# Perceiver megakernel, one core: PSUM banks of the first passes in two fixed sets, keys and values apart, one positive part on VectorE

## The chip, the cores and the metric

The kernel runs on one core of a Trainium2 chip. The metric is the device time of one execution in microseconds (us). Engines are named as the profile names them: PE (TensorE matmul) with PEld (its weight loads), DVE (VectorE), ACT (ScalarE), POOL (GpSimd), SP (the queue that issues most DMAs).

## The reference, cut to what matters

Four layers run one after the other on 128 tokens of width 256. Each has a cross attention over 12,544 context tokens of width 192, a self attention and a mixture of experts. The change lies in the cross attentions of the first three layers, all of this form (16 heads of width 16; the first has a mask, the second and third have biases, the second clips the scores):

```
q = (x @ Wq + bq)          # 128 x 256, in 16 heads
k = (context @ Wk + bk)    # 12544 x 256
v = (context @ Wv + bv)
scores = einsum(q, k) * scale
attn = softmax(scores, axis=-1)      # over 12544 keys
out  = einsum(attn, v);  x = x + out @ Wo + bo
```

## The kernel before, in words

`attend_twice` goes over the keys twice for each of two groups of eight heads: a first pass finds each row's highest score, a second pass (not touched) takes exponentials and weights the values. Three layers times two groups make six first passes.

A first pass has 25 steps, one for each pair of a pair of key blocks and a head half (a block is 512 context tokens, 25 blocks, the last half full). PE, DVE and ACT each keep the order in which the work is written down (`in_order`); POOL and SP do not. One step has four parts on PE, called K, V, O and H from here on:

- **K**: `keys.project(part 0)`, line 112: keys of a later block, 6 matmuls of 256 columns, on two row halves of the array.
- **V**: `keys.project(part 1)`, line 112: its values, 12 matmuls of 128 columns. After V, `keep` copies both out of PSUM: ACT takes the first half's keys and values (lines 145 or 147, 154), DVE the second half's (141 or 143, 152).
- **O**: `over`, line 641: queries times the difference of two key blocks (made by POOL, `apart`), 4 products of 512 columns t0 to t3, one on each 32-row quarter of the array. Line 672: ACT takes the positive part (Relu) of each into SBUF.
- **H**: `highest_of_two`, line 641, for the O of the step before: queries times the second block, 4 products. Line 678: DVE adds the positive part and keeps the maximum, four custom instructions ("customs").  With a mask (first layer), each H product begins with a bf16 matmul of a mask row (line 640).

So the highest of two blocks costs one maximum: max(a, b) = b + relu(a - b).

Which steps have K and V is set by `steps`. In the first layer and in every second group, almost every step projects a block; its last three projections have keys only (`values` is false for the last three blocks), the two steps after them have none. In the first group of the second and third layers eight blocks are there already, and every fourth step has no K and V. The values that are left out are projected at the end (`project_values`): those of block 22 just before the last H.

All of these products lie in one pool of 8 PSUM banks that go round (`single`: one bank of [128, 512] f32). A full step takes ten: K and V of a block share two (keys in the first half of each bank, values in the second), O four, H four. A matmul into a bank waits until the last reader of what lay there is done. Going round, this means in a full step: K's two banks are those of t0 and t1 of the O before; O's are those of t2 and t3 of the O before and t0 and t1 of the H before; H's are the last two of the H before and the K, V banks of its own step.

## Time and profile before

| | us |
|---|---|
| median of 3 runs (lowest, highest) | 3015.29 (3006.1, 3017.43) |
| the profiled execution's own time | 3019.33 |
| its span, first to last instruction | 3017.6 |
| PE busy in the span | 2877.8 |
| DVE busy | 2024.6 |
| ACT busy | 1691.3 |

The first passes lie, with what begins and ends them, in about 31 to 158, 281 to 410, 640 to 780, 915 to 1041, 1320 to 1455 and 1563 to 1693 us of the span: 787 us together, of which PE is busy for 766. Since matmuls are pipelined and their ends are modelled, that busy share says little on how near to its limit PE is; the distance from one O to the next tells the length of a step. It is read here in the timeline, from the first weight load of line 641 in a step, or from the first of the four rows of line 678.

### The profile page before, as it was taken

Reading aid. Unit: us, or ns where it says so; the run is one execution under the profiler, and the core shown is the slowest. Engines: PE = TensorE matmul, PEld = TensorE weight load, DVE = VectorE, ACT = ScalarE, POOL = GpSimd, SP = SyncE. Lnnn points to the kernel's source line nnn. Section 1 sums busy time; section 2 is a strip of 40 time slices with the busy share of each in tenths; the row PEclk is TensorE's granted clock in tenths of the full one; section 3 lists DMA queues with packets and bytes.
Section 4 is the critical chain, followed back from the end, with each engine's and each line's share of the span. In section 5 each row is a group of like instructions: output and inputs, shape, how many; then the busy total and the mean of one; then the engine's idle time right before and its main releaser. Section 6 shows DMA issues by size and latency. Waiting matters only on the chain.

```text
span 3017.6 us, 83446 instructions
## 1 busy us (share of the span) xinstructions
PE 2877.8 (95%) x36469; PEld 2250.9 (75%) x36469; DVE 2024.6 (67%) x3720; ACT 1691.3 (56%) x2326; POOL 288.4 (10%) x356
## 2 busy tenths in 40 slices
PE   8999999989999999899999998899999999999979
PEld 5677767456677676776777675688988989889858
DVE  4676677525895797657556655577777777777844
ACT  3577568234685585235775682355655656555521
POOL 4401420123001100121001002000000000000000
PEclk9999999899999998899999998999999999999979
DMA  5301310461002202431112007232223222222436
GB/s 156 92 19 42 108 34 26 175 224 53 21 3 76 68 5 87 132 117 48 32 34 76 27 4 261 87 97 83 85 78 88 85 78 88 81 82 84 135 115 199
DMA packets 149888, 255.32 MB, mean 85 GB/s; under 512 B 17892, under 2 KB 88159, under 8 KB 149524
## 3 DMA queue, kind: packets, MB, share of 16 engines
q1 hardware_dynamic: 144774, 235.01, 25.0%
q0 software_dynamic: 3744, 14.16, 1.5%
q8 instruction: 287, 4.70, 0.6%
q10 hardware_dynamic: 1006, 0.82, 0.1%
q14 instruction: 77, 0.63, 0.1%
HBM read 249.74 MB, written 0.19 MB: 83 GB/s over the span
## 4 chain that ended last, share of the span: by engine, by line
PE 74%; DVE 7%; ACT 2%; DMA 2%; POOL 1%; issue 1%; SPq 0%; DVEq 0%; POOLq 0%; ACTq 0%
PE acc L791 8%; PE pair L205 8%; PE one L641 8%; PE v L205 8%; PE one L112 7%; PE sc L949 6%; PE acc L991 5%; PE pair L721 5%; PE ps L329 4%; PE one L721 3%; PE acc L329 2%; PE pair L714 2%; PE kv L112 2%; PE ps L1787 1%; DVE sums L340 1%
## 5 line engine op out<-in xcount | busy, mean ns | idle before, releaser
L678 DVE CUSTOM_DVE_ANT_0 over<-over,one 128x512 f32<-128x512 f32 x576 | 361.0, 684 | 174.6 <-PE one L641 170.6
L672 ACT ACTIVATE over<-one 128x512 f32<-128x512 f32 x576 | 298.3, 602 | 92.5 <-PE one L641 84.8
L205 PEld LDWEIGHTS v<-wv,ctx 64*128 64x128 f32 (+1 forms) x3136 | 295.2, 190 | 12.0 <-issue 1.9
L205 PE MATMUL v<-wv,ctx 64*128 64x128 f32 (+1 forms) x3136 | 300.4, 274 | 0.0
L951 ACT COPY kept<-sc 128x1024 f32<-128x1024 f32 (+1 forms) x135 | 136.2, 1009 | 261.1 <-PE sc L949 261.1
L205 PE MATMUL pair<-ctx,wk 64*128 64x256 f32 (+1 forms) x1440 | 276.0, 384 | 1.2 <-ACT kT L233 1.1
L641 PE MATMUL one<-apart,qz 32*128 32x512 f32 x1536 | 246.6, 635 | 16.2 <-POOL apart L662 9.0
L340 DVE TENSOR_TENSOR top<-top,kept 128x1024 f32<-128x1024 f32 (+2 forms) x145 | 169.1, 1169 | 133.6 <-ACT kept L951 132.3
L343 DVE SCALAR_TENSOR_TENSOR e<-pair,floor 128x1024 f32<-128x1024 f32 x196 | 226.4, 1217 | 12.0 <-PE pair L721 12.0
L112 PEld LDWEIGHTS one<-ctx,wk 64*128 64x128 f32 x1464 | 156.9, 190 | 99.5 <-ACT over L672 84.7
L769 ACT ACTIVATE e<-pair 128x1024 f32<-128x1024 f32 x196 | 200.9, 1025 | 52.0 <-PE pair L721 29.8
L746 ACT ACTIVATE e<-e 128x1024 f32<-128x1024 f32 x196 | 207.4, 1058 | 33.1 <-DVE e L343 22.4
L721 PE MATMUL pair<-qz,kT 32*128 32x256 f32 x2112 | 218.9, 374 | 0.0
L205 PEld LDWEIGHTS pair<-ctx,wk 64*128 64x128 f32 (+1 forms) x1440 | 192.3, 188 | 34.1 <-issue 13.2
L112 PE MATMUL one<-ctx,wk 64*128 64x256 f32 x1464 | 214.8, 400 | 0.7 <-DVE o L340 0.7
L791 PE MATMUL acc<-e,v 128*17 128x128 f32 x6336 | 211.4, 274 | 3.0 <-ACT e L784 2.2
L112 PEld LDWEIGHTS one<-wv,ctx 64*128 64x128 f32 x2928 | 207.4, 193 | 8.8 <-ACT over L672 4.5
L112 PE MATMUL one<-wv,ctx 64*128 64x128 f32 x2928 | 208.3, 278 | 0.0
L791 PEld LDWEIGHTS acc<-e,v 128*17 128x17 f32 x6336 | 155.8, 97 | 67.8 <-ACT e L784 45.2
L784 ACT ACTIVATE e<-e 128x1024 f32<-128x1024 f32 x196 | 205.0, 1048 | 0.0
L343 DVE SCALAR_TENSOR_TENSOR e<-one,maskcol,less 128x256 f32<-128x256 f32 x392 | 162.6, 477 | 53.1 <-PE one L721 43.0
L949 PE MATMUL sc<-qz,kT 64*128 64x128 f32 x2816 | 197.8, 279 | 0.0
(479 smaller groups left out, 5271.7 us busy)
## 6 DMA issues: line engine op xcount, KB each, us to landing
ctx<-in_ctx SPq DMA_DIRECT2D x132, 384.0 KB
ctx<-in_ctxA SPq DMA_DIRECT2D x198, 256.0 KB
w<-in_L_ffn_W SPq DMA_DIRECT2D x32, 1024.0 KB
ctx<-in_ctxB SPq DMA_DIRECT2D x207, 128.0 KB
w<-in_L_ffn_w_gateT SPq DMA_DIRECT2D x8, 1024.0 KB
wu<-in_L_ffn_w_upT SPq DMA_DIRECT2D x8, 1024.0 KB
w<-in_L_ffn_w_downT SPq DMA_DIRECT2D x8, 1024.0 KB
w<-in_L_ffn_w1T SPq DMA_DIRECT2D x8, 1024.0 KB
```

Source lines behind the costliest of these rows:

```text
L112: self.nc.tensor.matmul(out, a, b, start=first, stop=last, skip_group_check=True)
L205: self.nc.tensor.matmul(out, a, b, start=start and not low, stop=low == 1, skip_group_check=True)
L343: self.nc.vector.scalar_tensor_tensor(out, a, s, b, op0, op1, **kw)
L641: nc.tensor.matmul(x, qz[r, g, s, :], k[r, :n], start=row is None, stop=True)
L672: nc.scalar.activation(e, x, AF.Relu)
L678: nc.vector.tensor_tensor_reduce(es[t], es[t], x, 1.0, -LARGEST, ALU.add, ALU.max, parts[:, s, t, i : i + 1])
L721: nc.tensor.matmul(at, keys.kT(c // 4)[tiles[t], k], q, start=start, stop=True, skip_group_check=True)
L746: nc.scalar.activation(to, to, AF.Exp)
L769: nc.scalar.activation(to, pair, AF.Exp)
L784: nc.scalar.activation(to, to, AF.Exp)
L791: nc.tensor.matmul(acc[32 * t : 32 * t + 17, half, :], v[:, c % 4 + j, 4 * half + t, :], es[half][:, t // 2, j, t % 2, :], start=c + j + h ...
L949: nc.tensor.matmul(x[:, t, c : c + P], kT[r, c : c + P], qz[r, g, :], start=True, stop=True)
```

## The change

1. The eight banks get fixed numbers and two sets of four, `free` (0 to 3 at first) and `taken` (4 to 7), which change parts after every step and after each of the blocks projected ahead. In a step, keys lie in the first two banks of `free`, values in the other two, O in the four of `taken`, and H in the four of `free` again. So after the change K and V wait for the four positive parts of the O before (K for t0 and t1, V for t2 and t3), O waits for the four customs of the H before (one each), and H for the copies of keys and values of its own step.
2. Keys and values have banks of their own, and both key copies go to ACT (`keep_keys`); they wait for K alone, no longer for V. DVE keeps one copy, that of the second half's values.
3. In steps that project something (`shared`), DVE takes the positive part of t1 with a `tensor_scalar` maximum with 0, in its order after the copy of values and before the customs; ACT takes three. Counted over the program, 124 of 576 positive parts move from ACT to DVE and 119 key copies of 128x256 move from DVE to ACT. PE, POOL and SP issue the same instructions as before, PE and POOL in the same order; on SP a load of a mask row and one of a context block change places.
4. Everything else that takes banks in the first pass (`project_values`, the last block's maxima, `lowered` and others) still goes round through all eight, with a counter of its own.

```diff
+    def keep_keys(self, g, b, p):
+        for i, _ in self.halves(b):
+            to, k = self.kT(b)[:, i * HB : (i + 1) * HB], p[:, i, :HB]
+            if self.bias is None:
+                self.nc.scalar.copy(to, k)
+            else:
+                self.nc.scalar.activation(to, k, AF.Identity, bias=self.bias[:, g : g + 1])
...
-            p = self.started[g, b] = self.net.early_two() if self.rest is None else self.net.two()
+            if self.rest is None:
+                p = self.net.early_two()
+            elif self.net.split:
+                p = self.net.banks_of(self.net.free[:2])
+            else:
+                p = self.net.two()
+            self.started[g, b] = p
             self.keys_into(p, g, b)
             return
         p = self.started[g, b]
-        if values:
-            self.values_into(p, g, b, HB)
-        self.keep(g, b, p, values=values)
+        if self.rest is not None and self.net.split:
+            if values:
+                v = self.net.banks_of(self.net.free[2:4])
+                self.values_into(v, g, b)
+            self.keep_keys(g, b, p)
+            if values:
+                self.keep(g, b, v, 0, keys=False)
+        else:
+            if values:
+                self.values_into(p, g, b, HB)
+            self.keep(g, b, p, values=values)
...
+        self.free, self.taken = list(range(4)), list(range(4, 8))
...
     def single(self):
+        if self.split:
+            self.next = (self.next + 1) % 8
+            return self.bank(self.next)
         return self.pone.tile([P, SB], F32, tag="one", name="one")
+
+    def bank(self, i):
+        return self.pone.tile([P, SB], F32, tag=f"one{i}", name="one", bufs=1)
+
+    def banks_of(self, at):
+        return Banks([self.bank(i) for i in at])
...
-            xs = [self.single()[:, :n] for _ in range(4)]
+            xs = [(self.single() if at is None else self.bank(at[t]))[:, :n] for t in range(4)]
...
-            for e, x in zip(out, products(g, 2 * i, s, less[0])):
-                nc.scalar.activation(e, x, AF.Relu)
+            for t, (e, x) in enumerate(zip(out, products(g, 2 * i, s, less[0], at=at))):
+                if shared and t == 1:
+                    self.ts(e, x, 0.0, None, ALU.max)
+                else:
+                    nc.scalar.activation(e, x, AF.Relu)
...
                 for b in range(lead):
                     for low in range(2):
                         keys.project(g, b, low)
+                    self.free, self.taken = self.taken, self.free
...
-                    es = over(g, i, s, less) if b < NSB - 1 else None
+                    es = over(g, i, s, less, self.taken, bool(steps[b])) if b < NSB - 1 else None
                     if before is not None:
-                        highest_of_two(g, *before, parts)
+                        highest_of_two(g, *before, parts, self.free)
+                    self.free, self.taken = self.taken, self.free
```

More of the change, by code (lines that the diff above doesn't have):

```diff
@@ L259, in __init__ @@
         self.banks = ExitStack()
-        self.turn = 0
+        self.turn = self.next = 0
+        self.free, self.taken = list(range(4)), list(range(4, 8))
         self.queue = self.nc.sync
@@ L632, in mask_rows, with products @@
             return row
-        def products(g, b, s, k, row=None):
+        def products(g, b, s, k, row=None, at=None):
             n = min(SB, S2 - b * SB)
-            xs = [self.single()[:, :n] for _ in range(4)]
+            xs = [(self.single() if at is None else self.bank(at[t]))[:, :n] for t in range(4)]
             for x, r in zip(xs, tiles):
@@ L663, in apart, with over @@
             return t[:, 0], t[:, 1], mask_rows(i)
-        def over(g, i, s, less):
+        def over(g, i, s, less, at, shared):
             out = []
@@ L670, in over, with highest_of_two @@
                 out += [e[:, j, :] for j in range(2)]
-            for e, x in zip(out, products(g, 2 * i, s, less[0])):
-                nc.scalar.activation(e, x, AF.Relu)
-            return out
-        def highest_of_two(g, i, s, less, es, parts):
-            for t, x in enumerate(products(g, 2 * i + 1, s, *less[1:])):
+            for t, (e, x) in enumerate(zip(out, products(g, 2 * i, s, less[0], at=at))):
[3 more added lines that the diff above has]
+                    nc.scalar.activation(e, x, AF.Relu)
+            return out
+        def highest_of_two(g, i, s, less, es, parts, at):
+            for t, x in enumerate(products(g, 2 * i + 1, s, *less[1:], at=at)):
                 nc.vector.tensor_tensor_reduce(
```

## The prediction

> **What bounds the kernel now.** I read the page first, then the chain in order of time over a stretch of the fourth first pass, then the timeline of one step, then that of a step without K and V. Passes are numbered 1 to 6 in order of time; 1 and 2 have the mask.

> From the page, the engines' totals:

> ```profile
> PE 2877.8 (95%) x36469; PEld 2250.9 (75%) x36469; DVE 2024.6 (67%) x3720; ACT 1691.3 (56%) x2326; POOL 288.4 (10%) x356
> ```

> The chain of work between 930 and 960 us (start, length, what):

> ```profile
> 930.20 3.03 PE one L112 x35
> 933.23 2.09 PE one L641 x16
> 935.32 3.03 PE one L112 x35
> ```

> It never leaves PE: 3.03 of K and V, 2.09 of O and H, 5.12 a step. But the chain has a wait inside it, which the timeline of the same pass shows (start, length, engine, what; in brackets idle time and who ended it):

> ```profile
> 938.28 0.31 PEld L641 LDWEIGHTS one<-apart,qz 32*128 32x128 f32 x8
> ...
> 938.79 0.41 DVE L152 COPY kv<-one 128x256 f32<-128x256 f32 x1
> ...
> 939.44 2.06 ACT L672 ACTIVATE over<-one 128x512 f32<-128x512 f32 x4 [0.52 <-PE one L641]
> 940.38 1.36 PEld L112 LDWEIGHTS one<-ctx,wk 64*128 64x128 f32 x12 [0.76 <-ACT over L672]
> ...
> 940.41 0.69 DVE L678 CUSTOM_DVE_ANT_0 over<-over,one 128x512 f32<-128x512 f32 x1 [1.20 <-PE one L641]
> ...
> 943.31 0.47 ACT L147 ACTIVATE kv<-one,bk 128x256 f32<-128x256 f32 x1 [1.80 <-PE one L112]
> 943.40 0.31 PEld L641 LDWEIGHTS one<-apart,qz 32*128 32x128 f32 x8
> ```

> The reader is to see: the next O comes 5.12 after this one; K is released by ACT's positive parts, t0 at 939.44 + 0.60 and t1 half a microsecond later; DVE copies values until 939.20, 0.92 after O began, which holds the last H products; ACT idles 1.80 while K and V run. Masked steps are also 5.12 long although PE has 0.21 more to do (mask rows at 58.29, H at 58.50). Equal lengths for unequal PE work mean that the ring O, positive part t1, K, V, O sets the step.

> What K and V take when nothing holds them, after a step without K and V:

> ```profile
> 1343.19 1.16 PEld L112 LDWEIGHTS one<-ctx,wk 64*128 64x128 f32 x12 [0.76 <-ACT over L672]
> ...
> 1346.02 0.31 PEld L641 LDWEIGHTS one<-apart,qz 32*128 32x128 f32 x8
> ```

> 2.83 from K to O, against 3.02 in the held step. And such a step itself, where DVE is the bound (customs 0.61 apart, 2.46 a step):

> ```profile
> 1340.71 0.18 PEld L641 LDWEIGHTS one<-apart,qz 32*128 32x128 f32 x1 [0.20 <-ACT over L672]
> 1340.72 0.18 PEld L641 LDWEIGHTS one<-kv,qz 32*128 32x128 f32 x1
> 1340.72 0.69 PE L641 MATMUL one<-kv,qz 32*128 32x512 f32 x1
> 1340.76 0.59 PE L641 MATMUL one<-apart,qz 32*128 32x512 f32 x1
> ```

> H's first product (kv) issues only when O's last (apart) has got its bank: PE takes its work in order. That matters below.

> **The change part by part.**

> *Full steps without mask.* K now waits for t0 on ACT and t1 on DVE at once. The DVE positive part is not in the trace; the nearest row has its form, 128x512 from PSUM:

> ```profile
> L347 DVE TENSOR_SCALAR floor<-one x4: 678/680/692, 788.6 to 1043.6; 128x512 f32<-128x512 f32 x4
> ```

> Started 1.16 after O (939.44 - 938.28), it ends at 1.84, and with 0.06 for the release (as from a custom's end to the next weight load, 1341.47 to 1341.53) K may go at 1.90. H is no longer held: values are copied by DVE alone until about 0.5. Unheld, O to K is the masked 2.15 (57.32 to 59.47) less the mask rows' 0.21, 1.94. So 1.94 + 2.83 = 4.77, a gain of 0.35. DVE: customs start at most at 2.13 as now, end 3 x 0.61 + 0.68 = 2.51 later, 4.64; O's t3 may go at 4.70, just ahead of 4.77. DVE's busy time, 0.35 + 0.61 + 2.43 = 3.4, and ACT's (two key copies for one and a positive part less, hidden in its 1.80 of idle time) stay below. Bounds: no gain at all, or 0.35. Passes 4 and 6 have 18 such steps each: 36 x 0.35 = -12.6.

> *Full masked steps.* 2.15 + 2.83 = 4.98; DVE's side, 2.35 (57.32 to 59.67) + 2.51 + 0.06 = 4.92, just below. A gain of 0.14 in 16 + 17 steps: -4.6.

> *Every fourth step without K and V (passes 3 and 5).* Here the new wait shows. O now waits for the customs of the H before, and H queues behind O on PE. With O at 0, customs from about 2.0 to 4.5, O's t3 goes at 4.57, K after it and H 1.94 later at 6.5, the next O at 9.33, where 2.46 + 6.13 = 8.59 stand now: +0.74. In pass 5 two full steps of each four give 0.70 back; in pass 3 one of these is held by POOL (`apart` behind `sums`, which waits for its load: 6.41 now), so only 0.35. Four rounds each: 0.2 + 1.6 = +1.8.

> *Steps with keys only or nothing, before the end of each pass.* From the last custom of one step to that of the next: 0.07 to O's t3, H's t0 beside it, 1.16 until its result (O's own), 2.51 of customs: 3.74, with mask 3.95. Keys-only steps take 3.8 today, empty ones 2.5 to 3.8. There are 5, 5, 6, 4, 6 and 4 in the six passes. Now they sum to 17.9 + 20.9 + 24.0 + 13.9 + 19.7 + 14.2 = 110.5, of which 7.7 are two stalls for other things that I leave; then 10 x 3.95 + 20 x 3.74 + 7.7 = 122. +11.4. Bounds: 0, if O or H is ready early, and this.

> *The second step of a pass.* K found fresh banks (919.01 O, 920.08 K: 1.07); now it waits for t1 until 1.90: +0.83 in passes 2 to 6 (pass 1 starts on its loads): +4.1.

> *Block 22's values.* They take two banks by the going-round counter. Counted through, in passes 4 to 6 one is that of t3 of the H just issued, so V (1.5) and the last H (1.16) start after the customs instead of beside them: 2.7 without DVE where 0.9 stand now, less 0.4 that the step before gave; +1.4 each. In passes 1 to 3 it is +0.7, -0.5 and -0.4. +4.0, between 0 and 8.

> *At no cost:* SP's exchange of two loads (no wait of PE on them in these steps), and POOL's `apart`, which is ready 2 us before its O in passes 1 and 4 to 6.

> The sum: -12.6 - 4.6 + 1.8 + 11.4 + 4.1 + 4.0 = **+4.1**. On the profiled execution's own 3019.3 that is 3023.4. This stands 4.0 above the median of the runs, so I predict **3019** for the median.

> *Weighed against the trace.* For the order on PE: the trace lets H's t0 start (1340.72) before the second half of O's t3 (1340.76), so two products share the array once both are issued. [...] For the clock: the granted clock is 1.00 in the stretches 933 to 1030 and 1336 to 1410, waits included. [...]

> **The rivals.**

> 1. *H gets past O in the short steps*, so that they stay as they are. For it: quarters of the array work side by side. Against it: the rows at 1340.7. The +1.8, +11.4 and +4.0, 17.2 together, fall to about a fifth: 3019 - 13.8 = 3005.
> 2. *Full steps come down further*, to about 4.55, because 0.2 between V and O, which no semaphore explains, belongs to the shared banks. For it: K and V follow each other without such a gap at the program's start. Against it: the gap is there also at 1346.02, where nothing was late. 69 full steps x 0.2 = 13.8: 3005, and with the first rival 2991.
> 3. *Full steps do not come down* (slower): the positive part on DVE is late and K's second bank trails, or K and V are slow for another cause than the wait. For it: PE counts as busy all through the step; K may go only 0.04 after t1. Against it: 2.83 when unheld. With unmasked steps of 5.0 instead of 4.77, 36 x 0.23 and some 3 in passes 3 and 5 are lost and the whole is slower by over 0.5%; at 5.12 everywhere the 17.2 of gain and 4 in passes 3 and 5 are lost: 3040.

> **How the numbers follow.** About 0.5%, 15 us, is what a measurement of this kernel can tell from no change. Forecast 0.52, mostly within it; first rival 0.12, on the edge; second 0.12, beyond; third 0.24. Faster 0.20, same 0.54, slower 0.26. The range goes from the first two rivals nearly together, 2994, to the third, 3038.

> **What would show it.** In pass 4 the distance between O's first weight loads: 4.77 (right), 5.1 (third rival), 4.55 (second). In pass 2: 4.98. The four customs of the last keys-only steps: 3.74 from step to step, with DVE idle 1.2 ahead of each first one, and PEld's wait ended by DVE line 715 (parts); 2.5 to 3.8 would be the first rival. K's wait in full steps ended by DVE's `tensor_scalar` (line 381) or by nothing. I would be wrong by more than the range if the clock fell below 1.00 in these passes, or if a wait that I do not see stood in each of the 98 or so full steps.

## The result and the profile after

| | us |
|---|---|
| before, median of 4 runs beside the changed kernel | 3016.28 (3006.1 to 3017.43) |
| after, median of 4 runs | 3063.18 (3056.82 to 3063.59) |
| ratio | 1.0158, 95% interval 1.0132 to 1.0184 |
| mean granted clock in the profiled execution, before and after | 0.969, 0.957 |

The changed kernel is 1.6% slower; the forecast was 3019, the range ended at 3038.

From the page of the changed kernel, the engines' totals:

```profile
PE 2896.3 (95%) x36469; PEld 2242.2 (73%) x36469; DVE 2066.5 (68%) x3725; ACT 1685.5 (55%) x2321; POOL 289.1 (9%) x356
```

PE's share is 95% as before. These totals do not tell what went wrong: PE counts as busy while it runs at half its clock (3.42 of 3.42 us in the last of the three stretches below, at a clock of 0.50).

A full step of the fourth pass in the timeline (start, length, engine, line; in brackets the idle time before and who ended it):

```profile
957.59 0.31 PEld L675 LDWEIGHTS one<-apart,qz 32*128 32x128 f32 x8
...
957.72 0.42 DVE L162 COPY kv<-one 128x256 f32<-128x256 f32 x1 [0.37 <-PE one L112]
...
958.79 0.69 DVE L381 TENSOR_SCALAR over<-one 128x512 f32<-128x512 f32 x1 [0.64 <-PE one L675]
...
959.52 1.18 PEld L112 LDWEIGHTS one<-ctx,wk 64*128 64x128 f32 x12 [0.76 <-ACT over L709]
...
959.61 0.69 DVE L715 CUSTOM_DVE_ANT_0 over<-over,one 128x512 f32<-128x512 f32 x1
...
962.36 0.31 PEld L675 LDWEIGHTS one<-apart,qz 32*128 32x128 f32 x8
```

This is as predicted to a few hundredths: O to K 1.93 (forecast 1.94), K to O 2.84 (2.83), a step 4.77 (4.77); in pass 2 it is 4.98 (4.98). The gain is there. The steps without K and V took the forecast wait too. One of them in pass 5, and the full step behind it:

```profile
1385.27 0.29 PEld L675 LDWEIGHTS one<-apart,qz 32*128 32x128 f32 x2 [1.60 <-DVE parts L715]
...
1387.64 2.57 PE L675 MATMUL one<-kv,qz 32*128 32x512 f32 x5
...
1390.13 2.21 PEld L112 LDWEIGHTS one<-ctx,wk 64*128 64x128 f32 x12 [1.50 <-ACT over L709]
...
1392.43 2.59 PEld L112 LDWEIGHTS one<-wv,ctx 64*128 64x128 f32 x24
```

O waits for the customs. But then H, K and V are slow: K's twelve weight loads take 2.21 (1.18 in the full step above), and the two steps take 12.6 from first custom to first custom, where the rounds beside them take 9.3. The stretches of 3.41 around it, which is the length of the shortest rows that the clock has in the traces, called windows below (length, then busy time and number of records of PE, PEld, DVE, ACT and POOL, then the granted clock, DMA share and GB/s):

```profile
1380.99:1384.40 3.41, 3.41 (x44) 2.15 (x40) 2.39 (x8) 1.95 (x5) 0.00 (x0) 1.00 0.23 46
1384.40:1387.81 3.41, 2.64 (x17) 1.54 (x15) 2.52 (x8) 2.19 (x5) 0.00 (x0) 1.00 0.18 74
1387.81:1391.23 3.42, 3.42 (x13) 1.26 (x10) 2.52 (x8) 1.03 (x2) 1.27 (x1) 0.50 0.01 2
```

A stretch with 17 PE records in place of 44, and from the next one on the clock is 0.50. Half clock is time with a granted clock of 0.50. Adding it up piece by piece, over three profiles of the changed kernel and two of the kernel before (means, us; passes are counted from their first custom to the first one of their last step):

| piece | before | after | longer by | half clock before | half clock after |
|---|---|---|---|---|---|
| start to first custom | 41.6 | 48.5 | 6.9 | 9.7 | 19.4 |
| passes 1 and 2 | 223.1 | 223.0 | -0.1 | 2.3 | 3.4 |
| pass 3 | 110.3 | 120.8 | 10.5 | 6.8 | 19.4 |
| between passes 3 and 4 | 149.9 | 156.2 | 6.3 | 1.7 | 13.7 |
| passes 4 and 6 | 224.2 | 219.0 | -5.2 | 0 | 1.6 |
| pass 5 | 105.1 | 120.5 | 15.3 | 2.6 | 25.5 |
| all other pieces | 2160.3 | 2171.9 | 11.6 | 164 | 182 |
| span | 3014.6 | 3059.7 | 45.2 | 187 | 265 |

The theory tested below (C): the waits are about what the prediction had, plus one that it overlooked at the start, and the larger part is the halved clock behind them. Its rival (W): the waits cost all of it, and the clock falls for another cause.

### The profile page after: what moved, and what is told of

Its sections match the earlier page's. It is cut to its first block, busy times and chain, and to the rows that moved or that the text cites. A ratio compares the mean times of both kernels' runs of the same rounds, so it can differ in the third digit from the quotient of the medians.

```text
span 3061.3 us, 83099 instructions
## 1 busy us (share of the span) xinstructions
PE 2896.3 (95%) x36469; PEld 2242.2 (73%) x36469; DVE 2066.5 (68%) x3725; ACT 1685.5 (55%) x2321; POOL 289.1 (9%) x356
## 4 chain that ended last, share of the span: by engine, by line
PE 85%; DVE 6%; DMA 3%; ACT 2%; POOL 2%; issue 1%; SPq 0%; POOLq 0%; DVEq 0%; ACTq 0%
PE one L112 11%; PE one L675 11%; PE acc L828 9%; PE v L229 8%; PE pair L229 8%; PE sc L988 6%; PE acc L1030 6%; PE pair L758 5%; PE ps L363 4%; PE one L758 4%; PE pair L751 2%; PE kv L112 2%; PE acc L363 2%; PE ps L1826 1%; DMA wu<-in_L_ffn_w_upT 1%
## 5 line engine op out<-in xcount | busy, mean ns | idle before, releaser
L709 ACT ACTIVATE over<-one 128x512 f32<-128x512 f32 x452 | 243.2, 598 | 130.8 <-PE one L675 114.6
L675 PE MATMUL one<-apart,qz 32*128 32x512 f32 x1536 | 269.7, 639 | 23.5 <-DVE parts L715 8.8
L112 PEld LDWEIGHTS one<-ctx,wk 64*128 64x128 f32 x1464 | 144.6, 194 | 115.8 <-ACT over L709 98.7
L112 PEld LDWEIGHTS one<-wv,ctx 64*128 64x128 f32 x2928 | 206.5, 200 | 15.2 <-DVE parts L715 4.4
L112 PE MATMUL one<-ctx,wk 64*128 64x256 f32 x1464 | 207.5, 409 | 9.8 <-DVE over L381 4.9
L112 PE MATMUL one<-wv,ctx 64*128 64x128 f32 x2928 | 208.3, 285 | 2.8 <-DVE parts L715 2.7
```

The lines of the kernel that those rows point to most:

```text
L112: self.nc.tensor.matmul(out, a, b, start=first, stop=last, skip_group_check=True)
L675: nc.tensor.matmul(x, qz[r, g, s, :], k[r, :n], start=row is None, stop=True)
L709: nc.scalar.activation(e, x, AF.Relu)
```

## Experiments

The kernel before, run beside each group of experiments, had medians of 3014.33 (1 to 4), 3012.01 (5 to 7) and 3012.95 (8 to 10), against 3016.28 beside the changed kernel; so differences of a few microseconds between groups tell nothing.

**1. The sets stay in place in steps without K and V.** O then takes the banks of the O before and no longer waits for customs.

```diff
+                    if not steps[b]:
+                        self.free, self.taken = self.taken, self.free
                     es = over(g, i, s, less, self.taken, bool(steps[b])) if b < NSB - 1 else None
```

> In a step without K and V the two sets of banks do not change parts: O takes the banks of the O before it, H those of the H before it, so O waits for positive parts alone and H for customs, which stand 0.61 apart. Everything else is as in the changed kernel (3063). Theory C, that PE's wait in these steps costs mostly through the granted clock: passes 3 and 5 lose the wait and the halved clock with it, so they take back most of the 10.9 and 15.0 that they had grown by, and some 3 of the wait itself; about 3063 - 27 = 3036, and the rows of half clock inside passes 3 and 5 (681.3, 701.7, 763.2; 1346.9, 1387.8, 1428.8) are gone. Theory W, that only the wait counts and the clock falls for another cause: two steps 9.34 become about 8.5, ten times, 3063 - 9 = 3054, with the half-clock rows still there.

Measured: 3024.57 (3016.0 to 3029.66, 10 runs), ratio to the kernel before 1.0033 (1.0019 to 1.0046). That is 38.6 less than the changed kernel, where W had 9. The stretches of pass 3 and pass 5:

```profile
667.10:780.80 113.70, 103.63 (x846) 66.33 (x846) 74.68 (x215) 56.21 (x117) 35.59 (x23) 0.94 0.16 45
1342.60:1447.10 104.50, 103.80 (x878) 68.97 (x878) 73.35 (x212) 56.91 (x118) 13.39 (x11) 0.97 0.19 55
```

Pass 5 is back at the length before (105.1) with full steps of 4.77, and a step without K and V and its follower take 2.44 + 6.04 = 8.48; the half clock in its rounds of these steps is gone. In pass 3 it is not: 13.7 is left (the clock of 0.94), where C had none, and the pass is 3 longer than before. Theory C had 3036, 11 too many. But the run tells C from W less well than these numbers suggest, for the edit took away more waits than the 9 of W: it also works in the steps without K and V at the end of each pass (3.78 to 2.44) and shortens the last step (6.55 to 4.62 in pass 4). The steps that are at full clock in both kernels are 15 shorter together, and the profile has 35 less of half clock, 14 at the price of 0.4 that experiment 4 gives: the larger part of what this edit won is waits. Experiment 2 is the one that tells the theories apart.

**2. The wait stays, and PE gets more to do in it**: products that nobody reads, into banks that the next H overwrites.

```diff
+                    if not steps[b] and before is not None:
+                        products(g, 2 * before[0] + 1, before[1], *before[2][1:], at=self.free)
```

> The wait of O for the customs stays, but PE first repeats the four products of the H before into the banks that the next H will overwrite, with nobody reading them, in each step without K and V. PE so has 0.96 more to do in a step where it stands idle for 0.77 to 1.5. Theory C: with more products in the window the clock is not halved, and the changed kernel gets faster by doing more: six events of about 3.3 less in passes 3 and 5, up to 0.3 lost in each of some 12 steps, about 3063 - 16 = 3047. Theory W: no gain, the added products cost 0 to 4: 3063 to 3067, with the half-clock rows where they were.

Measured: 3051.86 (3045.33 to 3055.37), 11.3 less than the changed kernel, by adding work; granted clock 0.9635 in the median of its four runs, 0.957 in those of the changed kernel. The windows that answer to those shown above:

```profile
1371.00:1374.41 3.41, 3.41 (x45) 2.25 (x41) 2.40 (x8) 1.95 (x5) 0.00 (x0) 1.00 0.24 38
1374.41:1377.83 3.42, 3.42 (x25) 2.19 (x23) 2.52 (x8) 2.15 (x5) 0.00 (x0) 1.00 0.20 79
1377.83:1381.24 3.41, 3.41 (x35) 2.28 (x31) 2.52 (x8) 1.65 (x4) 1.27 (x1) 1.00 0.01 2
```

25 records where there were 17, and the clock stays at 1.00. Every round of these steps in pass 5 now takes 3.88 + 5.45 = 9.33, with the wait still in it: the 12.6 were the clock. W had 3063 to 3067 and falls; the slowest of the four runs is below the fastest of the changed kernel (3056.82).

**3. ScalarE takes all four positive parts** (one part of the change undone).

```diff
-                    es = over(g, i, s, less, self.taken, bool(steps[b])) if b < NSB - 1 else None
+                    es = over(g, i, s, less, self.taken, False) if b < NSB - 1 else None
```

> ScalarE takes all four positive parts, as in the kernel before; banks and copies stay as in the changed kernel. By the working of the prediction, t1 is then ready at 2.10 after O instead of 1.90: full unmasked steps 4.93 or so instead of 4.77, 0.16 x about 45 = +7; masked ones hardly move. If the 6.0 lost ahead of the first custom is the DVE positive part that stands behind the DVE operation on the down weights, which waits for its load until 39.69, that goes: -5, and the first custom starts near 43 instead of 48.84. Together about 3065. If the 6.0 came from the new banks or from the clock alone, the first custom stays near 48.8 and the time is about 3070.

Measured: 3073.66 (3071.93 to 3077.92). The first custom starts at 40.60, so the lost time at the start is DVE's positive part. Full steps are 5.12, not the expected 4.93: K starts 1.93 after O, as in the changed kernel, but it takes 3.19 from K to O instead of 2.84, because K's second bank is that of t1, which now comes 0.49 after t0.

**4. ScalarE takes all four in the first two steps of the first pass only.**

```diff
-... self.taken, bool(steps[b])) if b < NSB - 1 else None
+... self.taken, bool(steps[b]) and not (masked and g == 0 and b < 2)) if b < NSB - 1 else None
```

> ScalarE takes all four positive parts in the first two steps of the first pass only; all else is the changed kernel. If the DVE positive part behind the load of the down weights is what cost 6.0 ahead of the first custom: first custom near 43, 3063 - 5.5 = 3057.5. If it was the clock or the banks: first custom near 48.8 and 3063.

Measured: 3050.19 (3043.04 to 3056.41), first custom at 41.43: 13 less where 5.5 was expected. Half clock fell with it (at the start 10.2 instead of 20.5, in the whole execution 243 instead of 264), part of it by luck, as pass 3 below shows. First the start in the changed kernel's timeline:

```profile
35.00 0.50 PEld L112 LDWEIGHTS one<-ctx,wk 64*128 64x128 f32 x2 [2.22 <-ACT over L709]
...
39.69 0.34 DVE L381 TENSOR_SCALAR down<-down,rate 32x256 f32<-32x256 f32 x1 [12.55 <-DMA down<-in_L_xattn_v_downT]
40.06 0.42 DVE L162 COPY kv<-one 128x256 f32<-128x256 f32 x1
40.40 0.68 DVE L381 TENSOR_SCALAR over<-one 128x512 f32<-128x512 f32 x1
41.14 1.78 PEld L112 LDWEIGHTS one<-ctx,wk 64*128 64x128 f32 x9 [5.64 <-DVE over L381]
```

and in this experiment:

```profile
34.24 2.27 PEld L112 LDWEIGHTS one<-ctx,wk 64*128 64x128 f32 x11 [2.24 <-ACT over L709]
...
38.69 0.34 DVE L381 TENSOR_SCALAR down<-down,rate 32x256 f32<-32x256 f32 x1 [12.54 <-DMA down<-in_L_xattn_v_downT]
```

DVE waits 12.5 for the load of the down weights in both. In the changed kernel the positive part stands behind it in DVE's order, and K, which needs the bank, stands still until 41.14; PE idles 4.92. This run gives one more comparison: its pass 3 is the same program as the changed kernel's, and happened to have no half clock at all:

```profile
662.00:775.10 113.10, 100.40 (x850) 62.88 (x846) 74.92 (x215) 58.14 (x117) 35.62 (x23) 1.00 0.15 46
```

113.1, against 118.2, 122.0 and 122.1 with 13.7, 20.5 and 23.9 of half clock in the three profiles of the changed kernel. A microsecond at half clock costs 0.37 to 0.43 here.

**5. Three edits together**: the first, the fourth, and at the end of each pass an order of the single banks in which those free longest come first (the seventh shows that edit alone).

```diff
+                    if not steps[b]:
+                        self.free, self.taken = self.taken, self.free
...
+... bool(steps[b]) and not (masked and g == 0 and b < 2)) if b < NSB - 1 else None
...
+            return self.bank((self.free + self.taken)[self.next])
```

> Three edits together on the changed kernel: the sets stay in place in steps without K and V; ScalarE takes all four positive parts in the first two steps of the first pass; and at the end of each pass the single banks are handed out in an order that takes the banks which have been free longest first (block 22's values go to two banks of the last O, the work of the next stage and the maxima of the last block to the banks of the H before). If the losses of the changed kernel are these three waits, with the clock that falls after them: 3024.6 (the first edit alone) less some 6 at the start and some 6 to 8 at the ends of passes, 3010 to 3013, while full steps stay at 4.77 and 4.98; that would be 0.1 to 0.2% below the kernel before. If the ends of passes are long for another cause (3.3 to 5.4 more behind passes 3, 4 and 6 than before), only the start is won: 3018.

Measured: 2998.12 (2996.52 to 3005.32), ratio to the kernel before 0.9963 (0.995 to 0.9975): faster than both kernels, and better than expected. Half clock is 181 in its profile, as low as in the kernel before (188 and 186).

**6. The positive part alone**: the kernel before, its ring of banks and its copies, with VectorE taking t1.

```diff
-            for e, x in zip(out, products(g, 2 * i, s, less[0])):
-                nc.scalar.activation(e, x, AF.Relu)
+            for t, (e, x) in enumerate(zip(out, products(g, 2 * i, s, less[0]))):
+                if shared and t == 1:
+                    self.ts(e, x, 0.0, None, ALU.max)
+                else:
+                    nc.scalar.activation(e, x, AF.Relu)
```

> The kernel before with one part of the change alone: VectorE takes t1 of the positive parts in steps with K or V (not in the first two steps of the first pass). Banks go round the ring and keys and values are copied by both engines as before. By the prediction's working the released bank is 0.16 to 0.20 earlier, and the 0.19 by which value copies on VectorE hold the last H stays: full unmasked steps 4.93 to 4.96 instead of 5.12, 36 x 0.17 + about 2 in passes 3 and 5 = -8, short steps as they are, no new half-clock rows: about 3007. If sets of banks are needed for the gain (K behind H's banks), or if the DVE part delays the customs and H by what it saves: 5.1 and 3015.

Measured: 3004.67 (2999.12 to 3008.98, 9 runs), ratio 0.9979 (0.9969 to 0.9989). Its full step in pass 4 (ACT's positive part is line 675 there):

```profile
947.31 0.31 PEld L641 LDWEIGHTS one<-apart,qz 32*128 32x128 f32 x8
...
949.44 1.16 PEld L112 LDWEIGHTS one<-ctx,wk 64*128 64x128 f32 x12 [0.76 <-ACT over L675]
...
952.27 0.31 PEld L641 LDWEIGHTS one<-apart,qz 32*128 32x128 f32 x8
```

O to K 2.13, as before (2.10); K to O 2.83 instead of 3.02: 4.96 a step. So the positive part on DVE alone is worth 0.16: it takes away the 0.19 by which K's second bank came late. With the banks and copies added, O to K falls from 2.13 to 1.93, the other 0.19. In experiment 3, with the banks and copies alone, steps stay at 5.12: what they gain ahead of K is lost behind it.

**7. Only the order of single banks at the ends of passes**, on the changed kernel: block 22's values go to two banks of the last O, and the last block's maxima begin with the banks of the H before.

```diff
-            return self.bank(self.next)
+            return self.bank((self.free + self.taken)[self.next])
...
+                    if b >= NSB - 2:
+                        self.next = -1 if b == NSB - 1 else 1
```

> The changed kernel with only the order of single banks at the end of each pass altered (block 22's values to two banks of the last O). Theory C: block 22's values no longer wait for customs, so the 0.7 of idle time goes, and with it the half clock under the small products behind it (20.5 at the end of pass 5, at times as long in pass 6): 1.4 in each of passes 4 to 6, some 4 to 5 of clock in pass 5, 0.9 to 1.9 for the maxima in passes 3 to 6: 3063 - 12 = 3051. If the clock falls there in any case (the small products give PE little to do), 3063 - 7 = 3056.

Measured: 3023.94 (3018.86 to 3031.71), 39 less, where C had 12. What it removed stands in the changed kernel's timeline at the end of pass 4:

```profile
1054.12 1.41 PEld L112 LDWEIGHTS one<-wv,ctx 64*128 64x128 f32 x16 [0.91 <-DVE parts L715]
...
1056.28 0.31 PEld L675 LDWEIGHTS one<-kT,qz 32*128 32x128 f32 x8 [0.75 <-DVE v L162]
...
1059.45 2.57 PEld L675 LDWEIGHTS one<-kT,qz 32*128 32x128 f32 x16 [2.86 <-DVE parts L715]
```

The second half of block 22's values waits for customs, the last H for its copies, and the first maximum of the last block for the last customs. In its place:

```profile
1035.77 1.42 PEld L112 LDWEIGHTS one<-wv,ctx 64*128 64x128 f32 x24 [0.76 <-ACT over L709]
...
1037.31 0.30 PEld L675 LDWEIGHTS one<-kT,qz 32*128 32x128 f32 x4
```

The last step of passes 4, 5 and 6 goes from 6.55, 15.00 and 9.38 to 3.51, 9.89 and 7.52. The granted clock rose from 0.957 to 0.967. In the kernel before, whose 42 executions differ by themselves between a clock of 0.963 and 0.974, 0.001 of clock goes with 1.9 us; by that 19 of the 39 are clock. By the length of half clock it is more: the profile is 43 shorter than the mean of the changed kernel's and has 77 less of it, 31 at 0.4, which leaves 12 for the waits, as many as C had for waits and clock together.

**8. More filling**: the second experiment's products, four more ahead of block 22's values, and twenty behind the first O of the first pass.

```diff
+                    if b == NSB - 2:
+                        products(g, 2 * i + 1, s, *less[1:], at=self.free)
+                    if masked and g == 0 and b == 0:
+                        for _ in range(5):
+                            products(g, 0, 0, less[0], at=self.taken)
```

> The changed kernel with all its waits, banks and copies, and only more products that nobody reads: four before O in each step without K and V (as in the second experiment), four before block 22's values at each end of a pass, twenty behind the first O of the first pass, where K waits for the positive part behind the load of the down weights (35.6 to 41.1). Theory C: the wait at the start and that for the customs stay, but the half-clock rows behind them go: against 3051.9 of the second experiment another 3 at the start and 5 to 15 behind passes 4 to 6, 3063 - 22 = 3041 or less, granted clock 0.967 or more instead of 0.957. Theory W: 3063 plus up to 5, with a clock of 0.957.

Measured: 3054.16 (3052.16 to 3056.26), with a clock of 0.968 in the median. The clock went where C had it, the time did not: the first custom starts at 54.04 instead of 48.84 (the twenty products run at half clock ahead of K, and half clock at the start stays at 20.5), and pass 2 is 118.6 long instead of 113.0. By 1.9 for 0.001, 11 in the clock are worth 21, so the added products cost 12. Filling shows a cause (experiment 2); it is no cure.

**9. A slower DVE in the kernel before**, two idle operations ahead of the customs in steps without K and V.

```diff
+                        if not steps[b]:
+                            for e in before[3][:2]:
+                                self.ts(e, e, 0.0, None, ALU.max)
```

> The kernel before, with two more VectorE operations (positive part again of t0 and t1, in place, which changes nothing) ahead of the customs in each step without K and V, so that VectorE, which bounds these steps, holds the next products some 0.7 longer; the banks go round as before. Some 16 such steps, 10 of them in the rounds of passes 3 and 5. Theory W: 16 x 0.7 = 11 at most, 3012 + 11 = 3023, the granted clock stays at 0.970. Theory C: the same 11, and where a 3.41 window now holds fewer than 15 products the clock halves behind it, 3.3 each, some six times: 3012 + 31 = 3043, clock about 0.962.

Measured: 3021.92 (3009.4 to 3027.52, 10 runs), ratio 1.0024 (1.0008 to 1.0039). Inconclusive: the edit did not make the wait that it was meant to make. Such a step and its follower took 4.22 + 4.36 = 8.58, as long as 2.46 + 6.13 before; the added time on DVE lay beside K's wait.

**10. The ring, the positive part on DVE, and all key copies on ACT**, keys and values still together in two banks.

```diff
-                if on_vector and self.bias is None:
-                    self.nc.vector.tensor_copy(to, k)
-                elif on_vector:
-                    self.nc.vector.tensor_scalar(to, k, self.bias[:, g : g + 1], None, ALU.add)
-                elif self.bias is None:
+                if self.bias is None:
```

> The kernel before with VectorE taking t1 of the positive parts (as in the sixth experiment) and with ScalarE copying all keys, so that VectorE has values of one half alone to copy; the banks go round the ring, keys and values stay together in two banks. If the 0.19 that is left between 4.96 and 4.77 is the values' copy on VectorE that holds the last H product, full unmasked steps come to 4.77 without sets of banks, 36 x 0.19 + some 2 in passes 3 and 5: 3005 - 9 = 2996, short steps as before, clock 0.969. If the sets are needed for it (O behind H's customs in the ring), the steps stay at 4.96 and the time at 3005.

Measured: 3053.16 (3051.43 to 3056.13): neither expectation. A full step of pass 4 is 5.61 (O and H are line 637 there):

```profile
972.53 0.31 PEld L637 LDWEIGHTS one<-apart,qz 32*128 32x128 f32 x8
...
973.26 0.49 ACT L143 ACTIVATE kT<-one,bk 128x256 f32<-128x256 f32 x1
...
973.78 0.42 DVE L148 COPY v<-one 128x256 f32<-128x256 f32 x1 [2.16 <-ACT kT L143]
...
974.26 0.29 PEld L637 LDWEIGHTS one<-kv,qz 32*128 32x128 f32 x2 [0.54 <-DVE v L148]
...
975.31 1.17 PEld L112 LDWEIGHTS one<-ctx,wk 64*128 64x128 f32 x12 [0.76 <-ACT over L671]
```

With keys and values of a half in one bank, DVE's copy of values comes only after ACT's copy of keys from the same bank (973.75, 973.78), and H behind both. In the changed kernel, where keys and values have banks of their own, ACT takes all keys at 4.77 a step; no run gave the ring such banks alone.

**11 to 14. Unaltered kernels once more**, for a second and third profile of the changed kernel and a second each of the kernel before and of experiment 7.

> The changed kernel unaltered, a second profile. If the half clock behind passes 4 and 6 (66.9 and 86.2 in the first) belongs to the change, it comes back within 5; if it hangs on where the free-running windows fall, it differs by 10 or more. The steps without full work in passes 3 and 5 have half clock in both cases, not necessarily in the same rounds; the wait at the start (K at 41.1) comes back.

> The changed kernel unaltered, a third profile; as for the second. At the start, passes 3 and 5 together I expect 40 to 75 of half clock (66 in the first), against 15 to 25 in the kernel before (23 in the first).

> The kernel before unaltered, a second profile: start, pass 3 and pass 5 with 15 to 25 of half clock together, passes 1, 2, 4 and 6 with under 5; behind passes 4 and 6 anything between 45 and 90 if these hang on the windows.

> The kernel of the seventh experiment unaltered, a second profile. If its 39 us were a true gain of the order of banks at the ends, the half clock behind passes 4 and 6 is low again (47.8 and 65.2 in the first); if 20 of them were luck of the windows, it is back at 60 and 80.

Measured: 3058.43, 3062.95, 3013.17 and 3031.46. Half clock at the start, in pass 3 and in pass 5 together: 66, 56 and 71 in the changed kernel, 22 and 16 in the kernel before. In each of the three, two of the four rounds of steps without K and V in pass 3 and two in pass 5 were hit; which ones, and whether any, was not the same in every execution: pass 3 of experiment 4 and of the first profile of experiment 7 had the same steps and not one round hit. That it hangs on where the windows fall is the author's reading. Between passes 3 and 4 it was 13.7, three times, against 3.4 and 0. The half clock behind passes 4 and 6 does not come back: 66.9, 76.9, 66.4 and 86.2, 89.7, 72.6 in the changed kernel, 58.0, 68.3 and 75.8, 86.6 before, 47.8, 64.9 and 65.2, 78.8 in experiment 7. Experiment 7's second profile is 13 longer than its first, and that is such luck (31 more of half clock behind these passes, 12 at 0.4): 30 below the mean of the changed kernel's profiles, where the first was 43 below.

## Why the prediction was wrong

Step by step, in its order:

- **Full steps**: right. 4.77 and 4.98 as forecast, and rivals 2 and 3 (4.55; 5.0 to 5.12) are out. Both halves of the 0.35 came out: O to K 1.93 for 1.94, K to O 2.84 for 2.83. Only the expectation of experiment 6 had the 0.16 of DVE's positive part ahead of K, where it came behind it.
- **Every fourth step without K and V**: the wait was right, 9.34 for two steps against the forecast 9.33, wherever the clock is whole. Where it is not, 12.6.
- **The second step of a pass**: right. In pass 4 K starts 1.87 after the first O instead of 1.07, +0.80 for +0.83.
- **Steps before the end of a pass**: right, 3.78 and 3.97 for 3.74 and 3.95, but for one in each pass of 4.22 (4.56 with mask). The thirty take 123 to 126 for the forecast 122. Rival 1 (H gets past O) is out.
- **Block 22's values**: +0.7, -0.5 and -0.4 in passes 1 to 3 exactly as counted (4.22, 4.22, 3.87 before; 4.89, 3.68, 3.51 after). In passes 4 to 6 it is +2.7, +4.8 and +1.8 in place of +1.4 each: the last H queues for the copies of values as well, and in pass 5 the small products behind it run at half clock (0.50 for 20.5 us from 1469.73 on in the first profile). The wait of the last block's maxima (2.86 above) was not in the sum.
- **"Pass 1 starts on its loads"**: this step failed. The DVE positive part was put at no cost there, but on DVE it stands behind an operation that waits 12.5 for a load; K waits 4.92 for it, and the first custom is 6.9 later with the clock (mean of the profiles). The rule that the prediction applied to PE's order, to ask what stands ahead in the queue, was not applied to DVE's.
- **The clock**: this is the step that cost most. The prediction read the granted clock in two stretches without trouble (1.00, 1.00). Its last sentence named a clock below 1.00 in these passes as what would put it wrong, and gave that no place in the sum. The trace of the kernel before has such a clock in pass 3, 0.97 over the whole stretch (640 to 780):

```profile
743.67:747.08 3.41, 3.41 (x12) 1.28 (x11) 3.41 (x12) 2.06 (x4) 1.27 (x1) 1.00 0.18 70
747.08:750.49 3.41, 3.41 (x14) 1.86 (x12) 1.79 (x6) 0.00 (x0) 0.00 (x0) 0.50 0.00 0
```

Windows of the kernel before: 12 PE records, and the next window at 0.50. In the same trace five windows of its passes 3 and 5 hold exactly 15 matmul records, counted as in the last section, and are followed by full clock. These steps stood at the edge: in all profiles none of 87 windows with 15 is followed by half clock, and 4 of 37 with 14 are (last section). A wait of 0.74 in each moved some of them below it; the window at 1384.40 above, with 17 PE records in place of 44, is one.

How much is clock: 78 more of half clock at 0.4 (pass 3 with and without it) is 31 of the 45 between the mean profiles; 0.0123 less in the clock at 1.93 for 0.001 (the kernel before's own executions) is 24. So 24 to 31 is clock, of which 57 x 0.4 = 23 sits in four pieces (the start, pass 3, between passes 3 and 4, pass 5) that had more of it in all three profiles. What is left, 14 to 21, are waits less the gain of the full steps: the net 4 that was forecast, 3 to 5 at the start, and the ends of passes. These last are not settled to better than a few microseconds, since behind each of them the clock changes too. Of the 24 to 31, 35 x 0.4 = 14 are in passes 3 and 5, where only some of the short steps have a window with fewer than 15 records.

## What to carry to other kernels

Before a change that adds waits on PE, count PE's matmuls in windows as long as the clock's shortest rows (3.41 us here), in the stages that the change touches, and find in the trace of before the count under which the clock has fallen; a stage that is near it can pay for a short wait twice (here two steps of 8.6 became 9.3 with the wait, and 12.6 where the clock fell as well). Give work to another engine only after looking at what stands ahead of it in that engine's order, at the first step of the program as much as in the steady one. When buffers change parts in a fixed rhythm, let steps that skip a part keep the parts as they were: here that exception, with one at the program's start and one at the ends of passes, turned a loss of 1.6% into a gain of 0.4%.

## What the runs showed of the hardware

The kernel before alone, 42 executions on several occasions, ran from 3004.9 to 3031.0 with clocks of 0.973 to 0.963, 13 of them on one occasion from 3009.5 to 3031.0. One and the same program so moves by up to 0.9% with the clock that it happens to get. That the place of the windows decides it fits the traces and was not tested by itself.
